# Graph attention on one core: own rows fetched earlier, and one slot in seven of layer 0 scored by two engines

## The chip, the cores and the metric

One Trainium2 chip; the kernel uses one of its cores. A core has TensorE (PE, the matrix engine; its weight loads are listed as PEld), VectorE (DVE), ScalarE (ACT), GpSimd (POOL, which here only issues indirect DMAs) and SyncE (SP, which issues plain DMAs). Each engine works off its own instructions in the order in which they were built. The metric is the device time of one execution in microseconds.

## The reference, cut to what matters

Eight batches of 2048 nodes with 256 channels pass two graph attention layers that share a sparse adjacency matrix; each layer's output is added to its input and normalised.

```python
# layer 0, leaky_relu slope 0.2
h1, h2, h3 = inp @ W1, inp @ W2, inp @ W3
e = einsum('bnd,bmd->bnm', h1, h2)
e = where(adj > 0, leaky_relu(e), -1e12)
x = layernorm(x + relu(softmax(e) @ h3))
# layer 1: e[n, m] = leaky(e_src[n] + e_dst[m]) with 4 heads of 64, elu in place of relu
```

A node has some 17 neighbours of 2048, so the kernel gathers neighbour rows and never forms the full matrix. With A = W1 W2ᵀ the logit of node n and neighbour m is (x[n] A) · x[m], and the weighted sum is taken over rows of x, and multiplied by W3 afterwards.

## The kernel before, in words

**Units.** The nodes are sorted by degree and cut into 16 tiles of 128. The batches are taken in two halves of four. One tile of one half in one layer is a *unit*: 32 units for layer 0 (first half, tiles 15 down to 0, then the second half), 32 for layer 1. A unit of tile t has K = `SLOTS[t]` neighbour slots, from 12 (tile 15) to 36 (tile 0, which is cut into two parts of 18); the 32 units of layer 0 have 596 slots.

**What is done for a layer 0 unit.**
- `list_job` and `neighbours` (first half only) turn a row of the adjacency matrix into indices.
- `chunk_job` gathers neighbour rows, `gather` being an indirect DMA issued by POOL (L196), one for each slot: 128 rows of 4 x 256 float32 into a ring `s` of 16 buffers with two slots each. A buffer is free when PE has used its second slot.
- `before0` gathers the unit's own rows into `xo`, a pool of two buffers. SP copies them to `xr`, a pool of three buffers, for the residual (L531); PE transposes them (`transposed`, L417), ACT copies the transpose out of PSUM (L419), PE multiplies by A (`projected`, L427), and ACT copies the result to `g` (L542).
- `logits0` makes, for each slot and each of the four batches, one dot product of a 256-element row with `g`. It is one DVE instruction with a sum (L562), which the profile shows as two, the product and a read of the accumulator. After all slots of a part come the leaky relu (L575), the mask, the maximum (L580), the subtraction (L581), the exponential on ACT (L582), the sum (L585) and the division (L588).
- `sums0` makes, for each slot, four diagonal matrices on ACT (`dg`, L659; four buffers of them) and lets PE multiply the slot's rows by them, accumulating in PSUM (`add_slot`, L639).
- `after0` copies the sum out (`hs`, L674), transposes it (L417, L419), multiplies by W3, adds the residual (DVE, L699), normalises (statistics on DVE, L384; logarithm and exponential of `z` on ACT, L395 and L396; L407), stores, and projects for layer 1 (L723, L731).

All PSUM tiles other than the accumulators come from one pool, `ps`, of four buffers: transposes, projections, and small things.

**Order.** Python generators are advanced by `tick`: each tick first issues what gathers the ring allows, then takes up to two steps of the logits of a later unit, then of the starts (`before0`), ends (`after0`) and lists. POOL runs in exactly that order (`manual_schedule` for Pool). The order of the other engines' instructions is set by the scheduler of the tile framework, from dependencies and its own estimates, when the program is built; on the chip each engine then keeps it. While unit j is summed, the logits of unit j+1 are made, and the start of unit j+3 is queued when half of unit j is summed:

```python
for share in sums[u.layer](u):
    ahead[0] -= share
    left -= share
    tick(left + units[min(j + 1, len(units) - 1)].K + LEAD)
    if not begun and left <= u.K / 2 and j + 3 < len(units):
        begun = True
        v = units[j + 3]
        starts.append(before[v.layer](v))
```

The lines of layer 1 that the profile names are L774 to L886 and L840 and are not touched by the change.

Of the kernel before, what the change touches and what calls it, by code (L numbers as in the profile page):

```python
# [11 lines left out]
F32 = mybir.dt.float32  # L12
BF16 = mybir.dt.bfloat16
# [3 lines left out]
AF = mybir.ActivationFunctionType  # L17
ALU = mybir.AluOpType
# [4 lines left out]
P = 128  # L23
# [106 lines left out]
def fast_path(  # L130
# [24 lines left out]
    nc = tc.nc  # L155
    B, N, C = x.shape
    NT = N // P
    KC = C // P
    HB = B // 2
    HC = HB * C  # L160
    HG = HB * H
    HW = HC // 2
# [7 lines left out]
    xop = ctx.enter_context(tc.tile_pool(name="xown", bufs=2))  # L170
# [7 lines left out]
    sp = ctx.enter_context(tc.tile_pool(name="small", bufs=4))  # L178
# [3 lines left out]
    def ps_tile(name):  # L182
        return ps.tile([P, 512], F32, tag="ps", name=name)
# [4 lines left out]
    def ring_tile(name):  # L188
        return ring.tile([P, CHUNK * 2 * QW], F32, tag="ring", name=name)

    def wide_tile(name):
        return wp.tile([P, 2 * QW], F32, tag="t", name=name)

    def gather(dst, table, index):

        nc.gpsimd.indirect_dma_start(  # L196
            out=dst, out_offset=None, in_=table, in_offset=AT(ap=index, axis=0),
            bounds_check=table.shape[0] - 1, oob_is_err=False,
        )
# [12 lines left out]
    xg = [tc.dram_tile([N, HC], F32, name=f"xg_{h}") for h in range(2)]  # L212
# [18 lines left out]
    for it in range(NT):  # L231
        r = ring_tile(f"adj_{it}")
# [54 lines left out]
    for it in range(NT):  # L287
        if it % 2 == 0:
            nc.vector.tensor_scalar(
                junk1, keys, key[:, it : it + 1], 0.0, ALU.is_gt, ALU.add,  # L290
                accum_out=rank[:, it : it + 1],
# [23 lines left out]
    order = const.tile([P, NT], I32, tag="order", name="order")  # L315
# [15 lines left out]
    for r in range(2):  # L331
        rr = slice(64 * r, 64 * r + 64)
        pr = ps_tile(f"ps_half_{r}")[:, :NT]
# [78 lines left out]
    def transposed(src, name, dst):  # L412

        for i in range(2):
            pt = ps_tile(f"ps_t_{name}_{i}")
            for j in range(4):
                nc.tensor.transpose(pt[:, ts(j, P)], src[:, ts(4 * i + j, P)], ident)  # L417
            yield
            nc.scalar.copy(dst[:, ts(i, 512)], pt)  # L419
        yield  # L420

    def projected(srcT, weight, name, evict):
        for i in range(2):
            pp = ps_tile(f"ps_p_{name}_{i}")
            for j in range(2):
                for k in range(KC):
                    nc.tensor.matmul(  # L427
                        pp[:, ts(j, C)],
                        lhsT=srcT[:, ts((2 * i + j) * KC + k, P)],
                        rhs=weight[:, k, :],  # L430
                        start=(k == 0),
                        stop=(k == KC - 1),
                    )
            yield
            evict(i, pp)
        yield

    class Unit:
        def __init__(self, layer, h, t):
            self.layer, self.h, self.t = layer, h, t  # L440
            self.K = SLOTS[t]
            self.name = f"{layer}_{h}_{t}"

            n = self.K if self.K <= RING * CHUNK * 3 // 4 else -(-self.K // 2)
            self.parts = [(k, min(n, self.K - k)) for k in range(0, self.K, n)]
            self.chunks = [[] for _ in self.parts]
            self.p = [None] * len(self.parts)
            self.ps = [None] * len(self.parts)

            self.m, self.s = [], []  # L450
            self.ready = False


# [68 lines left out]
        listed[t] = True  # L522


    def before0(u):
        xo = xop.tile([P, HC], F32, tag="xo", name=f"xo_{u.name}")
        gather(xo, xg[u.h][:, :], order[:, u.t : u.t + 1])
        u.xr = xrp.tile([P, 2, HW], F32, tag="xr", name=f"xr_{u.name}")
        for r in range(2):
            for c in range(2):  # L530
                nc.sync.dma_start(  # L531
                    u.xr[64 * c : 64 * c + 64, r, :], xo[64 * r : 64 * r + 64, ts(c, HW)]
                )
        for _ in range(4):
            yield
        xT = wide_tile(f"xT_{u.name}")
        yield from transposed(xo, f"x_{u.name}", xT)
        while scored[0] < u.index - 1:
            yield
        u.g = gp.tile([P, HC], F32, tag="g", name=f"g_{u.name}")  # L540
        yield from projected(
            xT, w.A, f"g_{u.name}", lambda i, pp: nc.scalar.copy(u.g[:, ts(i, 512)], pp)  # L542
        )
        u.ready = True

    def logits0(u):

        while not u.ready:
            yield 0
        for i, (k0, K) in enumerate(u.parts):  # L550
            n, o = f"{u.name}_{i}", offs[u.t] + k0
            e = ep.tile([P, HB, K], F32, tag="e", name=f"e_{n}")
            for k in range(K):
                c, s = divmod(k, CHUNK)
                while len(u.chunks[i]) <= c:
                    yield 0
                while clock[0] < u.chunks[i][c][2] + 3:
                    yield 0
                rows = u.chunks[i][c][0]
                for b in range(HB):  # L560
                    jt = sp.tile([P, C], BF16, tag="j", name=f"j_{n}_{k}_{b}", bufs=1)
                    nc.vector.tensor_tensor_reduce(  # L562
                        out=jt,
                        in0=rows[:, s, ts(b, C)],
                        in1=u.g[:, ts(b, C)],
                        scale=1.0,
                        scalar=0.0,
                        op0=ALU.mult,
                        op1=ALU.add,
                        accum_out=e[:, b, k : k + 1],  # L570
                    )
                yield 1
            p = e
            wide = [P, HB, K]
            nc.vector.scalar_tensor_tensor(p, e, ALPHA, e, ALU.mult, ALU.max)  # L575
            nc.vector.tensor_tensor(
                p, p, neg[:, o : o + K].unsqueeze(1).to_broadcast(wide), ALU.add
            )
            m = sp.tile([P, HG], F32, tag="m1", name=f"m_{n}")[:, :HB]
            nc.vector.tensor_reduce(m, p, AX.X, ALU.max)  # L580
            nc.vector.tensor_tensor(p, p, m.unsqueeze(2).to_broadcast(wide), ALU.subtract)  # L581
            nc.scalar.activation(p, p, AF.Exp)  # L582
            yield 0
            sm = sp.tile([P, HG], F32, tag="s1", name=f"s_{n}")[:, :HB]
            nc.vector.tensor_reduce(sm, p, AX.X, ALU.add)  # L585
            if len(u.parts) == 1:
                nc.vector.reciprocal(sm, sm)
                nc.vector.tensor_tensor(p, p, sm.unsqueeze(2).to_broadcast(wide), ALU.mult)  # L588
            u.m.append(m)
            u.s.append(sm)  # L590
            u.p[i] = p
            yield 0
# [321 lines left out]
    units = [Unit(0, h, t) for h in range(2) for t in up]  # L914
# [19 lines left out]
    for j, u in enumerate(units):  # L934
        u.index = j
    before = (before0, before1)
    logits = (logits0, logits1)
    sums = (sums0, sums1)
    after = (after0, after1)
# [7 lines left out]
    def finish(u):  # L947
        yield from after[u.layer](u)
# [6 lines left out]
    def tick(limit):  # L955
        pump()
        while late and late[0][0] <= clock[0]:
            late.popleft()[1]()
        for _ in range(2):
            if ahead[0] < limit:  # L960
                ahead[0] += next(stream, 0)
        for queue in queues:
            for _ in range(min(len(queue), 2)):
                if queue and next(queue[0], queue) is queue:
                    queue.popleft()
        clock[0] += 1
# [5 lines left out]
    for j, u in enumerate(units):  # L972
        begun = False
        if 0 < j and j + 2 < NT:
            lists.append(neighbours(up[j + 2]))
        if j == NT:
            ends.append(checks())
        while len(ends) > 1:
            tick(0)
        if 2 <= j < 10:  # L980
            b, i = divmod(j - 2, 2)
            n = ts(i, N // 2)

            nc.gpsimd.dma_start(xg[1][n, ts(b, C)], x[HB + b, n])
        left = float(u.K)
        for share in sums[u.layer](u):
            ahead[0] -= share
# [6 lines that stand above are left out]
        ends.append(finish(u))  # L994
# [300 lines left out]
```

## Time and profile before

| | us |
|---|---|
| median of 5 runs (lowest to highest) | 2593.92 (2588.98 to 2598.82) |
| time of the profiled execution | 2593.16 |
| its span, from the first to the last instruction | 2591.0 |
| busy: PE / DVE / ACT / POOL | 1807.5 / 2148.8 / 1442.3 / 1538.1 |
| granted TensorE clock, mean | 0.856 |

The stages by time in the span: preparation up to about 110 us; layer 0, first half of the batches, from 110 to about 850; layer 0, second half, to about 1600; layer 1 to the end. Inside each half the units grow from 12 slots to 36. Busy time in six stretches:

| stretch (us) | length | PE | DVE | ACT | POOL |
|---|---|---|---|---|---|
| 0 to 110 | 110 | 13.2 | 74.8 | 52.4 | 38.2 |
| 110 to 300 | 190 | 133.0 | 171.2 | 93.9 | 111.5 |
| 300 to 820 | 520 | 424.3 | 472.1 | 320.8 | 289.3 |
| 820 to 900 | 80 | 57.3 | 62.5 | 45.6 | 38.0 |
| 900 to 1400 | 500 | 405.6 | 375.1 | 298.6 | 238.0 |
| 1400 to 1600 | 200 | 158.1 | 156.0 | 128.5 | 113.0 |

How the views are read. A line of the *groups* view gives line, engine, operation, output and input tiles, shapes and count; then the busy time of all, the mean of one in ns, and the idle time of the engine just ahead of them with what ended it. A line of the *waits* view reads "engine and line <- what it waited for: us in total, times, longest us". In the *timeline* a line is start, duration, engine, instruction, and in brackets the idle time before it with what ended that. "issue" means that the profile shows no wait.

### The profile page before, as it was taken

The page shows a single profiled execution, that of the slowest core. Times are in us where ns is not written, and L with a number is a line of the kernel's source. Part 1 is how long each engine was busy: PE and PEld are TensorE (multiplying, and loading weights), DVE is VectorE, ACT ScalarE, POOL GpSimd, SP SyncE. Part 2 cuts the span into 40 slices and gives each one's busy share as a digit, 9 for nine tenths or more (in the row PEclk, how much of TensorE's full clock was granted, in tenths as well). Part 3 has the DMA queues.
Part 4 walks back from the last instruction along what each step waited for, and adds up shares of the span by engine and source line. Part 5 has one row for each costly group of instructions (what it writes and reads, how often), then busy time and mean ns, then how long its engine had stood idle before and what let it go on. Part 6 is the DMA issues. An engine that isn't in the chain of part 4 may idle for free. (4 is left out here: it accounts for less than half of the span.)

```text
span 2591.0 us, 52231 instructions
## 1 busy us (share of the span) xinstructions
PE 1807.5 (70%) x16675; PEld 984.7 (38%) x16675; DVE 2148.8 (83%) x7073; ACT 1442.3 (56%) x4849; POOL 1538.1 (59%) x1486
## 2 busy tenths in 40 slices
PE   1168787878778788787888878756465666664674
PEld 0145454545555455454555544222121212221221
DVE  6799799899989776777788885788888788888896
ACT  6246475656566555565666656554356546643455
POOL 3475455555555443545455565677677777776774
PEclk9578898989889898898898989878788788887877
DMA  9897787888885676767787868898899999987993
GB/s 383 274 339 271 258 310 266 298 292 275 290 276 185 211 225 212 266 225 241 247 263 275 268 202 281 306 354 298 294 349 348 344 335 364 349 315 270 330 350 110
DMA packets 249419, 734.92 MB, mean 284 GB/s; under 512 B 63200, under 2 KB 72544, under 8 KB 246704
## 3 DMA queue, kind: packets, MB, share of 16 engines
q0 software_dynamic: 192512, 645.89, 70.6%
q1 hardware_dynamic: 55360, 84.44, 9.6%
q8 instruction: 135, 2.21, 0.3%
q10 hardware_dynamic: 1264, 1.18, 0.1%
q14 instruction: 148, 1.21, 0.1%
HBM read 708.35 MB, written 76.09 MB: 303 GB/s over the span
## 5 line engine op out<-in xcount | busy, mean ns | idle before, releaser
L562 DVE CUSTOM_DVE_ANT_0 j<-s,g 128x256 bf16<-128x256 f32 x2384 | 1007.8, 423 | 195.0 <-DMA s<-xg,idx 125.7
L196 POOL DMA_INDIRECT s<-xg,idx x596 | 637.5, 1070 | 617.4 <-PE acc L639 393.3
L639 PE MATMUL acc<-s,ident 64*64 64x512 f32 x4768 | 607.7, 660 | 355.0 <-issue 298.0
L639 PE MATMUL acc<-s,dg 64*64 64x256 f32 x9536 | 701.6, 416 | 184.1 <-ACT dg L659 173.0
L196 POOL DMA_INDIRECT s<-qg,idx x596 | 610.5, 1024 | 241.0 <-issue 132.5
L659 ACT ACTIVATE dg<-twice,e 128x64 f32<-128x64 f32 x2384 | 617.2, 337 | 105.3 <-PE acc L639 99.2
L840 DVE TENSOR_TENSOR s<-s,p 128x2048 f32<-128x2048 f32 (+1 forms) x260 | 574.1, 2230 | 0.0
L639 PEld LDWEIGHTS acc<-s,dg 64*64 64x64 f32 x9536 | 380.3, 143 | 445.3 <-ACT dg L659 253.5
L639 PEld LDWEIGHTS acc<-s,ident 64*64 64x64 f32 x4768 | 207.9, 149 | 747.3 <-issue 596.7
L836 ACT ACTIVATE s<-s,e 128x64 f32<-128x64 f32 x1408 | 342.6, 334 | 49.3 <-DVE e L804 38.9
L395 ACT ACTIVATE z<-st,roots 128x4 f32<-128x4 f32 x64 | 19.1, 298 | 404.2 <-DVE st L384 404.2
L562 DVE DVE_READ_ACCUMULATOR2_ANT e<- 128x1 f32 x2384 | 194.2, 81 | 0.0
L204 POOL DMA_INDIRECT out_dram<-o,oidx x128 | 129.3, 1010 | 66.7 <-ACT o L407 31.2
L774 DVE TENSOR_TENSOR e<-s,own 128x32 f32<-128x32 f32 (+1 forms) x306 | 56.0, 186 | 121.4 <-DMA s<-qg,idx 118.2
L417 PE MATMUL ps_t_x<-ident,xo 128*128 128x128 f32 x256 | 55.5, 359 | 126.5 <-DMA xo<-xg,order 126.5
L723 PE MATMUL ps_q<-wqs,x1T 128*128 128x264 f32 x512 | 136.3, 403 | 0.7 <-ACT x1T L419 0.7
L427 PE MATMUL ps_p_h<-w_sb,hT 128*128 128x256 f32 x512 | 130.2, 398 | 6.1 <-ACT hT L419 6.1
L427 PE MATMUL ps_p_g<-A,xT 128*128 128x256 f32 x512 | 130.9, 401 | 0.1
L427 PEld LDWEIGHTS ps_p_h<-w_sb,hT 128*128 128x128 f32 x512 | 94.2, 194 | 41.5 <-issue 13.3
L407 ACT ACTIVATE o<-xr,nmr,rstd 128x256 f32<-128x256 f32 x128 | 66.5, 589 | 77.4 <-DVE nmr L403 69.8
L427 PEld LDWEIGHTS ps_p_g<-A,xT 128*128 128x128 f32 x512 | 97.7, 199 | 29.8 <-issue 8.5
L723 PEld LDWEIGHTS ps_q<-wqs,x1T 128*128 128x128 f32 x512 | 97.5, 197 | 27.8 <-issue 7.3
(138 smaller groups left out, 1472.6 us busy)
## 6 DMA issues: line engine op xcount, KB each, us to landing
adj<-in_adj_dram SPq DMA_DIRECT2D x16, 1024.0 KB
xr<-xo SPq DMA_DIRECT2D x128, 128.0 KB
x1s<-y SPq DMA_DIRECT2D x32, 512.0 KB
xr<-x1s SPq DMA_DIRECT2D x32, 512.0 KB
s<-xg,idx POOLq DMA_INDIRECT x596
s<-qg,idx POOLq DMA_INDIRECT x596
edges<-adj SPq DMA_DIRECT2D x16, 512.0 KB
xg<-in_x_dram SPq DMA_DIRECT2D x4, 2048.0 KB
```

The source lines that it names most:

```text
L196: nc.gpsimd.indirect_dma_start(out=dst, out_offset=None, in_=table, in_offset=AT(ap=index, axis=0), bounds_check=table.shape[0] - 1, oob_i ...
L204: ins = nc.gpsimd.indirect_dma_start(out=table, out_offset=AT(ap=index, axis=0), in_=src, in_offset=None)
L407: nc.scalar.activation(dst[:, b, :], y[:, b, :], AF.Identity, bias=nmr[:, b : b + 1], scale=rstd[:, b : b + 1],)
L417: nc.tensor.transpose(pt[:, ts(j, P)], src[:, ts(4 * i + j, P)], ident)
L427: nc.tensor.matmul(pp[:, ts(j, C)], lhsT=srcT[:, ts((2 * i + j) * KC + k, P)], rhs=weight[:, k, :], start=(k == 0), stop=(k == KC - 1),)
L562: nc.vector.tensor_tensor_reduce(out=jt, in0=rows[:, s, ts(b, C)], in1=u.g[:, ts(b, C)], scale=1.0, scalar=0.0, op0=ALU.mult, op1=ALU.add, ...
L639: nc.tensor.matmul(out, lhsT=lhsT, rhs=rhs, start=(k == 0 and j == 0), stop=(k == K - 1 and (j == 1 or diag is None)), tile_position=(64 * ...
L659: nc.scalar.activation(diag[:, b, :], twice, AF.Copy, scale=u.p[i][:, b, k : k + 1])
L723: nc.tensor.matmul(pq[:, : C + 2 * H], lhsT=x1T[:, ts(i * KC + k, P)], rhs=w.sqs[:, k, j * H : j * H + CD + H], start=(k == 0), stop=(k == ...
L774: nc.vector.tensor_tensor(e[:, c * CHUNK : c * CHUNK + ns, :].rearrange("p s (b g) -> p s b g", b=HB), rows[:, :ns, :].rearrange("p s (b w ...
L836: nc.scalar.activation(v[:, a, g, :], v[:, a, g, :], AF.Copy, scale=pv[:, a, g : g + 1])
L840: nc.vector.tensor_tensor(v, v, pv.unsqueeze(3).to_broadcast([P, n * HB, H, D]), ALU.mult)
```

## The change

Two edits, both in layer 0. First, the gather of a unit's own rows moves out of `before0` into a function of its own, `own_rows`, that the main loop calls for unit j+3 ahead of the first sum of unit j, where `before0` was queued at the middle of unit j. Everything else of `before0` stays there. The first three units still gather in `before0`. Second, for slots 3, 10, 17 (`k % 7 == 3`) of each part, DVE no longer makes four dot products with a sum; it makes two plain products of 512 elements into two PSUM tiles of the pool `ps`, and ACT reads them in four copies of 256 elements whose accumulator output is the sum.

```diff
+    def own_rows(u):
+        u.xo = xop.tile([P, HC], F32, tag="xo", name=f"xo_{u.name}")
+        gather(u.xo, xg[u.h][:, :], order[:, u.t : u.t + 1])
+
     def before0(u):
-        xo = xop.tile([P, HC], F32, tag="xo", name=f"xo_{u.name}")
-        gather(xo, xg[u.h][:, :], order[:, u.t : u.t + 1])
+        if u.xo is None:
+            own_rows(u)
+        xo = u.xo
...
                 rows = u.chunks[i][c][0]
+                if k % 7 == 3:
+
+                    for r in range(2):
+                        pr = ps_tile(f"pr_{n}_{k}_{r}")
+                        nc.vector.tensor_tensor(
+                            pr, rows[:, s, ts(r, HW)], u.g[:, ts(r, HW)], ALU.mult
+                        )
+                        for j in range(2):
+                            b = 2 * r + j
+                            ja = sp.tile([P, C], BF16, tag="ja", name=f"ja_{n}_{k}_{b}", bufs=1)
+                            nc.scalar.activation(
+                                ja, pr[:, ts(j, C)], AF.Copy, accum_out=e[:, b, k : k + 1]
+                            )
+                    yield 1
+                    continue
                 for b in range(HB):
...
             nc.gpsimd.dma_start(xg[1][n, ts(b, C)], x[HB + b, n])
+        if j + 3 < 2 * NT:
+
+            own_rows(units[j + 3])
         left = float(u.K)
```

By the built order 86 of the 596 slots take the new way: 344 pairs of DVE instructions go, 172 products and 344 ACT sums come. On POOL an own-rows gather stands 6 to 18 slot gathers earlier than before (for most units 7 to 12), except for the fourth unit, whose gather now stands first of all POOL's gathers, ahead of the first adjacency list. On PE the transposes of the own rows keep their places among the sums to within a slot, except in the third and fourth unit.

More of the change, by code (lines that the diff above doesn't have):

```diff
@@ L450, in __init__ @@
             self.m, self.s = [], []
+            self.xo = None
             self.ready = False
```

## The prediction

> **What bounds the kernel now.** I read the busy time by stretches first, then the waits of PE, DVE and ACT inside two of them, then the timeline at one wait. Layer 1 (1600 us to the end) keeps its order on every engine, so what is at stake lies between 95 and 1600 us.
>
> Two stretches; the columns are window, length, then busy time and count of PE, PEld, DVE, ACT, POOL, then clock and DMA share:
>
> ```profile
> 300.00:820.00 520.00, 424.30 (x4401) 275.31 (x4400) 472.07 (x2267) 320.81 (x1126) 289.30 (x272) 0.89 0.81 275
> 900.00:1400.00 500.00, 405.60 (x3928) 264.26 (x3928) 375.06 (x1708) 298.58 (x997) 237.99 (x227) 0.91 0.73 242
> ```
>
> The waits in 300 to 820 us:
>
> ```profile
> ACT z L395 <- DVE st L384: 104.3, 12, 13.5
> PE acc L639 <- ACT dg L659: 85.2, 19, 9.7
> ACT dg L659 <- PE acc L639: 33.5, 30, 1.9
> ACT e L582 <- DVE e L581: 33.4, 10, 10.1
> DVE j L562 <- DMA s<-xg,idx: 15.9, 20, 1.7
> PE ps_t_x L417 <- DMA xo<-xg,order: 10.3, 3, 4.6
> ```
>
> DVE is busy 91% and leads: ACT stands 138 us waiting for DVE's statistics and logits, PE stands 85 us behind ACT. This stretch is **bound by DVE**.
>
> The waits in 900 to 1400 us:
>
> ```profile
> DVE j L562 <- DMA s<-xg,idx: 91.1, 58, 7.3
> PE ps_t_x L417 <- DMA xo<-xg,order: 60.9, 12, 7.0
> ACT dg L659 <- PE acc L639: 49.3, 43, 1.9
> ACT z L395 <- DVE st L384: 43.8, 11, 7.0
> PE acc L639 <- ACT dg L659: 36.5, 26, 3.4
> ```
>
> Here DVE is busy only 75%, and waits for gathered rows; these wait for ring buffers that PE frees. PE's 405.6 busy, 60.9 waiting for own rows and 36.5 for diagonals make 503 of 500 us: nothing else is in PE's time. This stretch is **bound by PE's queue**, with 12% of it spent on own rows that came late. One such wait:
>
> ```profile
> 1007.52 1.04 POOL L196 DMA_INDIRECT xo<-xg,order  x1 [0.30 <-issue]
> ...
> 1016.37 1.09 PE L417 MATMUL ps_t_x<-ident,xo 128*128 128x128 f32 x4 [5.86 <-DMA xo<-xg,order]
> ```
>
> POOL issues the gather at 1007.5; PE, in order, has been standing before the transposes for 5.9 us when the rows are there 8.9 us after the issue.
>
> **Edit 1, own rows earlier.** PE waits 126.5 us for `xo` in all, 21 times. The first two (13.9 and 24.6 us, at 109 and 140 us) are the start-up, whose gathers are not moved ahead; 88.0 us are left: 60.9 in 900 to 1400, 10.3 in 300 to 820, some 13 in 110 to 300, 4 after 1400. At its new place a gather stands right behind one that POOL issued, in 900 to 1200, 20 to 28 us before the old `xo` issue (979.7 against 1007.5, for example); the longest of these waits is 7.0, so all should go. POOL must then wait for the buffer: for the four copies to `xr` of the unit two before. In this trace those stand at least 11 us ahead of the new places (963.5 against 979.7 here), so behind it on POOL nothing is held. The moved gather takes its 1.04 + 0.30 us of POOL either way.
>
> What is worth how much: in 900 to 1400, with 60.9 us less, DVE's 375 us stand in 439 (85%), so DVE and the diagonals get part of it; I take 50. In 300 to 820 DVE hides PE's waits: 5 of 10.3. Elsewhere 8 of 17. Together **-63**, bounds 0 and -88. At the start, the fourth unit's gather now stands ahead of the first list: 1.3 us of POOL and 512 KB, 1.5 us at the 350 GB/s of that stretch, on the path to the first index: **+2** (0 to 3).
>
> **Edit 2, on DVE.** Rows (groups by form; busy, mean ns | idle before):
>
> ```profile
> L562 DVE CUSTOM_DVE_ANT_0 j<-s,g 128x256 bf16<-128x256 f32 x2384 | 1007.8, 423 | 195.0 <-DMA s<-xg,idx 125.7 <-ACT g L542 5.4
> ...
> L731 ACT COPY q<-ps_q 128x264 f32<-128x264 f32 x128 | 48.0, 376 | 31.6 <-PE ps_q L723 31.1
> ...
> L680 ACT ACTIVATE hs<-acc,fs 128x256 f32<-128x256 f32 x8 | 3.1, 474 | 4.7 <-DVE fs L622 4.7
> L258 ACT ACTIVATION_READ_ACCUMULATOR junk<-adj 128x1 f32 x16 | 3.0, 186 | 0.0
> ...
> L873 DVE TENSOR_TENSOR v<-v,v 128x512 f32<-128x512 f32 x4 | 2.7, 684 | 0.0
> ```
>
> A dot with its accumulator read starts every 0.43 (busy time over count, 300 to 820) to 0.47 us (timeline at 1002): 1.72 to 1.87 for a slot. A product of 512 takes 684 ns, 0.64 (L867, 8 in 5.1 us busy) to 0.68 from one to the next; writing to PSUM costs hardly more (L799, 128x304 into PSUM, 483 ns; L789, same size into SBUF, 476). So 1.28 to 1.37 in its place, 0.35 to 0.6 saved, I take 0.5, x86 = 43 us. It counts where DVE leads: 43 of the 86 slots lie in 300 to 820 and after 1400, **-22** (0 to -52).
>
> New waits of DVE. By the built order 94 of the 172 products wait for ACT to free a PSUM tile, so many of slot 10's and 17's products stand at the end of their part; in 4 of the 34 parts nothing at all lies between them and the leaky relu, in some 8 more only one or two dots. There DVE waits while ACT sums: four sums of 0.6 less the second product, 2 us; about 20 us in all, dots and lists queued behind. Some 8 of it falls where DVE leads: **+8** (0 to +30). At the turn to the second half, the products of slot 10 of unit (1, tile 14) now stand behind the statistics and checks (about 885 us); its exponential was at 862, its first diagonal at 893.4. With ACT's sums it is late next: **+5** (0 to +12).
>
> **Edit 2, on ACT.** No row has 256 elements from PSUM with an accumulator. Lower bound 0.37 + 0.19 (L731 and the read), upper 0.47 + 0.19 (L680 and the read): 0.56 to 0.66, I take 0.6; x344 = 206 us more ACT. In 900 to 1400, 27 slots, 65 us: 49.3 us of ACT's waiting for PE to free a diagonal absorb most, the rest delays diagonals that PE waits for: **+20** (0 to +65). In 300 to 820, 33 slots, 79 us: taking each sum's new place in ACT's order and the times of its neighbours in this trace, DVE would deliver the product some -1 to +14 us after ACT gets there, in the middle 1.7. So ACT waits, sums 2.4 us, and the diagonals behind come later; PE has slack to DVE there: **+10** (0 to +30).
>
> [...]
>
> **Sum.** -63 + 2 - 22 + 8 + 5 + 20 + 10 = -40 on the profiled 2593.16 (2591.0 of span and 2.2 around it), so 2553. The median of the runs, 2593.92, lies 0.8 above: 2554.
>
> **Rivals.**
> - *Both in full* (15%). The own-row waits go entirely (-88 + 2), DVE's 22 count, ACT's sums hide in its idle 40%: 2485 with no new wait at all, 2510 with those of DVE at +13 and of ACT at +12. For it: PE's account of 900 to 1400 is complete, ACT is idle enough. Against: ACT's idle time is waiting in order, not free room.
> - *The wait moves* (12%). What PE no longer waits for rows it waits for diagonals (36.5 us in that stretch already) or DVE becomes the bound there: 63 shrinks to 20, 2596 in the sum; if the ACT terms are half as well, 2581. Between: about 2589. Against: DVE and ACT are at 75% and 60% there.
> - *ACT becomes the bound: slower* (22%). Place: diagonals behind the sums. In 300 to 820 ACT has 321 busy + 79 + 138 waiting for DVE = 538 of 520 if its waits for DVE stay whole, and in 900 to 1400 all 65 fall on PE: +18, +65, and 10 slots after 1400 +12, with the waits of DVE at +25 and +5, against -63 + 2 - 22: 2635 at worst; with three quarters of the first three, 2611, which I take. It decides once more than 60% of those 95 us are felt.
> - *It doesn't do what it says* (4%): the scheduler's buffer wait holds the own rows as late as before; only edit 2 stays, about 2600. The order on POOL speaks against it.
>
> **How the numbers follow.** My forecast (47%) is 2554, its own range 2527 to 2583. The range that should hold 8 in 10 takes in most of "both in full" and the near part of "slower": 2505 to 2612. A measurement of this kernel can tell about 0.2% (5.2 us) from no change. Faster: 47 + 15 + 5 of "moves" = 67%; same: 6 + 2 = 8%; slower: 22 + 1 + 2 = 25%.
>
> **What would show it.** Edit 1: the wait of PE for `xo` falls from 126.5 to about 40 us, and DVE's wait for rows in the second half shrinks with it. Edit 2: L562 falls by 344 pairs; the products show 0.69 us, the sums 0.37 to 0.47 with a read of 0.19; DVE gains a wait for ACT at the leaky relu of 10 to 30 us; PE's wait for `dg` grows from 173 by less than 40. I am wrong if that wait grows by 80 or more, if ACT's waits for products are as long as the sums themselves, or if POOL waits for `xr` copies ahead of own rows.

## The result and the profile after

| | before | after |
|---|---|---|
| median, us (runs) | 2591.7 (78) | 2596.66 (41) |
| lowest to highest | 2579.55 to 2602.5 | 2586.47 to 2605.0 |
| span of the profiled execution | 2591.0 | 2591.2 |
| busy DVE / ACT | 2148.8 / 1442.3 | 2104.6 / 1566.8 |

The ratio is 1.0018, with a 95% interval of 1.0011 to 1.0025: 0.2% slower, where 2554 had been forecast. The two profiled executions are equally long, but inside they are not alike. The table follows the end of each unit's last diagonal on ACT (us from the start, from the traces):

| unit (half, tile) | before | after | difference |
|---|---|---|---|
| (0, 15) | 174.7 | 180.6 | +5.9 |
| (0, 7) | 500.0 | 511.4 | +11.3 |
| (0, 3) | 685.2 | 717.9 | +32.8 |
| (0, 0) | 854.3 | 894.6 | +40.3 |
| (1, 12) | 1011.5 | 1035.9 | +24.3 |
| (1, 6) | 1282.4 | 1276.6 | -5.7 |
| (1, 0) | 1588.5 | 1590.6 | +2.1 |

So 40 us are lost in the first half, most of it in its large units, 46 are won between the turn and unit (1, 6), and 8 are lost again in the large units at the end.

The windows of the profile after, for the same two stretches (length, then busy time and count of PE, PEld, DVE, ACT, POOL, then clock, DMA share and GB/s):

```profile
300.00:820.00 520.00, 419.40 (x4080) 259.62 (x4075) 426.40 (x1949) 350.81 (x1301) 268.02 (x255) 0.93 0.78 269
900.00:1400.00 500.00, 424.62 (x4159) 272.58 (x4163) 390.95 (x1668) 355.22 (x1306) 260.19 (x245) 0.93 0.78 261
```

Between 300 and 820 us no engine is fuller than before but ACT: DVE fell from 472.1 to 426.4, and less was done in that time (PE's matmuls 4401 to 4080). Between 900 and 1400 all engines are busier.

Since less was done between 300 and 820, the same work has to be compared: from the end of unit (0, 12) to that of (0, 1), first before, then after, each with DVE's wait for rows in it.

```profile
290.80:785.60 494.80, 403.70 (x4124) 263.26 (x4127) 447.18 (x2146) 306.76 (x1071) 275.06 (x259) 0.89 0.83 286
DVE j L562 <- DMA s<-xg,idx: 18.5, 21, 1.9
...
299.70:822.90 523.20, 422.61 (x4112) 261.30 (x4108) 428.34 (x1958) 353.43 (x1312) 269.16 (x256) 0.93 0.78 268
DVE j L583 <- DMA s<-xg,idx: 70.2, 43, 7.6
```

These units take 28.4 us longer. DVE is busy 18.8 us less in them and waits 51.7 us longer for gathered rows.

The waits of the kernel after in 300 to 820 us:

```profile
ACT ja L576 <- DVE pr L570: 109.7, 29, 10.4
DVE j L583 <- DMA s<-xg,idx: 68.2, 42, 7.6
PE acc L660 <- ACT dg L680: 42.4, 42, 3.6
ACT dg L680 <- PE acc L660: 15.6, 16, 1.9
ACT z L395 <- DVE st L384: 10.9, 7, 3.9
```

The first line is new: ACT stands before a sum whose product DVE has not made, 3.8 us each time. DVE's wait for gathered rows was 15.9 and is 68.2, so that DVE loses more to waiting than it saves in work. The wait for own rows is gone.

The same in 900 to 1400 us:

```profile
DVE j L583 <- DMA s<-xg,idx: 59.0, 44, 5.0
ACT ja L576 <- DVE pr L570: 58.8, 27, 4.6
PE acc L660 <- ACT dg L680: 48.9, 31, 3.7
ACT z L395 <- DVE st L384: 28.7, 10, 5.9
ACT dg L680 <- PE acc L660: 13.5, 16, 4.7
```

Here the 60.9 us of PE's wait for `xo` are gone, and DVE's wait for rows fell from 91.1 to 59.0, as forecast.

The groups by form show each operation at the price that was forecast (busy, mean ns | idle before):

```profile
L576 ACT ACTIVATE ja<-pr 128x256 bf16<-128x256 f32 x344 | 130.9, 380 | 251.5 <-DVE pr L570 248.9
...
L570 DVE TENSOR_TENSOR pr<-s,g 128x512 f32<-128x512 f32 x172 | 112.8, 693 | 14.1 <-DMA s<-xg,idx 9.5 <-ACT q L752 4.4
...
L576 ACT ACTIVATION_READ_ACCUMULATOR ja<-pr 128x1 f32 x344 | 68.5, 199 | 0.0
```

What was not forecast stands behind the last bar of the first line: 248.9 us of ACT waiting for products, more than the 199 that the sums take.

The timeline of the kernel after around two such stops, while unit (0, 3) is summed and the logits of (0, 2) are made (start, duration, engine, instruction, idle time before it with its cause):

```profile
675.51 0.38 ACT L576 ACTIVATE ja<-pr 128x256 bf16<-128x256 f32 x1 [10.44 <-DVE pr L570]
...
678.17 1.11 PE L417 MATMUL ps_t_h<-ident,hs 128*128 128x128 f32 x4 [10.94 <-ACT hs L695]
...
681.50 0.99 POOL L196 DMA_INDIRECT s<-xg,idx  x1 [10.21 <-PE acc L660]
...
688.72 0.43 DVE L583 CUSTOM_DVE_ANT_0 j<-s,g 128x256 bf16<-128x256 f32 x1 [7.64 <-DMA s<-xg,idx]
...
691.57 1.29 DVE L570 TENSOR_TENSOR pr<-s,g 128x512 f32<-128x512 f32 x2
692.29 0.38 ACT L576 ACTIVATE ja<-pr 128x256 bf16<-128x256 f32 x1 [4.35 <-DVE pr L570]
...
694.57 4.11 PE L660 MATMUL acc<-s,dg 64*64 64x256 f32 x32 [2.29 <-ACT dg L680]
```

Read it as a ring. ACT, in order, has stood 10.44 us before a sum whose product was late, with the copies of `hs` (677.53) and the next diagonals (678.48) behind it. PE therefore stands 10.94 us at the transposes of `hs`. POOL's gather has waited 10.21 us for a ring buffer that PE frees, and goes out at 681.50. Its rows, by the count of the slots, are those for which DVE stands 7.64 us, until 688.72. So DVE's next product is late too, ACT stands again, 4.35 us, and PE 2.29 us behind it.

### The profile page after: what moved, and what is told of

Its sections match the earlier page's. It is cut to its first block, busy times and chain, and to the rows that moved or that the text cites. A ratio compares the mean times of both kernels' runs of the same rounds, so it can differ in the third digit from the quotient of the medians.

```text
span 2591.2 us, 52332 instructions
## 1 busy us (share of the span) xinstructions
PE 1827.5 (71%) x16675; PEld 972.3 (38%) x16675; DVE 2104.6 (81%) x6557; ACT 1566.8 (60%) x5537; POOL 1535.4 (59%) x1486
## 5 line engine op out<-in xcount | busy, mean ns | idle before, releaser
L583 DVE CUSTOM_DVE_ANT_0 j<-s,g 128x256 bf16<-128x256 f32 x2040 | 862.3, 423 | 218.7 <-DMA s<-xg,idx 166.9
L660 PE MATMUL acc<-s,dg 64*64 64x256 f32 x9536 | 722.1, 410 | 154.8 <-ACT dg L680 144.3
L680 ACT ACTIVATE dg<-twice,e 128x64 f32<-128x64 f32 x2384 | 631.3, 342 | 36.3 <-PE acc L660 35.3
L576 ACT ACTIVATE ja<-pr 128x256 bf16<-128x256 f32 x344 | 130.9, 380 | 251.5 <-DVE pr L570 248.9
L395 ACT ACTIVATE z<-st,roots 128x4 f32<-128x4 f32 x64 | 19.0, 296 | 256.0 <-DVE st L384 255.9
L744 PE MATMUL ps_q<-wqs,x1T 128*128 128x264 f32 x512 | 143.2, 417 | 36.6 <-ACT q L752 13.5
L583 DVE DVE_READ_ACCUMULATOR2_ANT e<- 128x1 f32 x2040 | 166.2, 81 | 0.0
L744 PEld LDWEIGHTS ps_q<-wqs,x1T 128*128 128x128 f32 x512 | 99.1, 202 | 70.3 <-ACT q L752 15.9
L570 DVE TENSOR_TENSOR pr<-s,g 128x512 f32<-128x512 f32 x172 | 112.8, 693 | 14.1 <-DMA s<-xg,idx 9.5
```

The costliest lines, as they stand in the source:

```text
L570: nc.vector.tensor_tensor(pr, rows[:, s, ts(r, HW)], u.g[:, ts(r, HW)], ALU.mult)
L576: nc.scalar.activation(ja, pr[:, ts(j, C)], AF.Copy, accum_out=e[:, b, k : k + 1])
L583: nc.vector.tensor_tensor_reduce(out=jt, in0=rows[:, s, ts(b, C)], in1=u.g[:, ts(b, C)], scale=1.0, scalar=0.0, op0=ALU.mult, op1=ALU.add, ...
L660: nc.tensor.matmul(out, lhsT=lhsT, rhs=rhs, start=(k == 0 and j == 0), stop=(k == K - 1 and (j == 1 or diag is None)), tile_position=(64 * ...
L680: nc.scalar.activation(diag[:, b, :], twice, AF.Copy, scale=u.p[i][:, b, k : k + 1])
L744: nc.tensor.matmul(pq[:, : C + 2 * H], lhsT=x1T[:, ts(i * KC + k, P)], rhs=w.sqs[:, k, j * H : j * H + CD + H], start=(k == 0), stop=(k == ...
```

## The experiments

Theory: **the wait in order.** ACT's stops before products tie PE's diagonals of this unit to DVE's logits of the next, and PE's ring buffers tie DVE to PE. Rivals: ACT's added **time** by itself; the PSUM **tiles** that products hold; a loss by **edit 1**. Two groups ran on two slower chips: on that of a1_own, a2_split and a4_short before takes 2700.65 us, on that of c0_before to b2_second 2702.07. So all are compared by their ratio to before on the same chip (95% interval in brackets).

**Own rows alone, the split alone, and short sums**

```diff
 a1_own: without the split
-                if k % 7 == 3:
...
 a2_split: without the early gather
-        if j + 3 < 2 * NT:
-            own_rows(units[j + 3])
 a4_short: both edits
-                                ja, pr[:, ts(j, C)], AF.Copy, accum_out=e[:, b, k : k + 1]
+                                ja[:, :8], pr[:, j * C : j * C + 8], AF.Copy, accum_out=e[:, b, k : k + 1]
```

> Edit 1 alone: own rows ahead, all slots by DVE's dots. Theory (the two edits work against each other: own rows gain in the second half, edit 2 loses as much in the large units of the first half): 2540 to 2555, the sums of unit (first half, tile 0) end within 6 us of before (854 us), those of (second half, tile 6) some 45 us earlier than before (1282 us); PE's waits for own rows fall to about 45 us. Rival (own rows ahead cost the first half by pushing neighbour gathers back): the first half ends 25 us or more late in this kernel too, and the time is 2580 or more.

> Edit 2 alone: one slot in seven by DVE's products and ACT's sums, own rows as before. Theory: slower, 2630 to 2645, and the first half's sums end 30 to 45 us later than before; PE's waits for own rows stay over 100 us. Rival (the loss in the first half is edit 1's): 2585 to 2600 and the first half ends within 10 us of before.

> Both edits, but ACT sums only the first 8 of 256 elements of each batch, so the logits of those slots are wrong; all waits, tiles and instruction counts stay, ACT has some 0.2 us less for each of 344 sums, 70 us in all. If ACT's time is what the change loses by: 2570 or less. If the waits in ACT's order (for DVE's products) and for PSUM tiles are: within 12 us of both edits together, 2585 to 2600, with ACT's wait for products as long as or longer than the 249 us there.

Measured: own rows alone 0.9851 (0.9827 to 0.9876), the split alone 1.014 (1.0118 to 1.0161), short sums 0.9995 (0.998 to 1.001). The product of the first two is 0.999: the change is a gain of 1.5% and a loss of 1.4%. The short sums with their reads still take 127.9 us of ACT, where the full ones take 199.4; the third that is gone bought at most 0.4%. So this bounds the price of the sums' length only loosely: by it, all 199 us could be worth up to some 1.1% (an estimate, 0.4% times 199 over 71). The split alone missed two of its marks: PE waited 80.8 us for own rows, where over 100 was expected, and the first half ended 17 us later than in the trace of c0_before, where 30 to 45 was expected.

**Before and after on the second slower chip, sums one slot later, and the split in the second half only**

```diff
 b1_late: the sums are issued behind the next slot's dots
-                            nc.scalar.activation(
-                                ja, pr[:, ts(j, C)], AF.Copy, accum_out=e[:, b, k : k + 1]
-                            )
+                        late.append((k, r, pr))
...
+                if late:
+                    summed(n, e, late)
 b2_second
-                if k % 7 == 3:
+                if u.h == 1 and k % 7 == 3:
```

> The kernel before, unchanged, for a trace from the chip on which the next kernels run. The marks of the units of layer 0 (the end of each unit's last diagonal on ACT) should stand as in the first trace, apart from one factor for the chip. If the loss of some 40 us by the end of the first half (854 to 895 us in the first two traces) is a property of the kernels and not of one execution, it must show against the changed kernel here too.

> The changed kernel, unchanged, beside the others of this group. Ratio to before 1.002 (0.999 to 1.005). Against the trace of before from this chip: some 30 to 40 us late at the end of the first half, all of it caught up in units (1, tile 12) to (1, tile 6), a few us late after the last units of layer 0.

> Both edits, but ACT's sums of a product are issued one slot later, behind the next slot's dots in program order (at once if it is the last slot of its part). Theory of order: what edit 2 costs is that ACT stops in order before a product that DVE has not yet made (249 us of waits), with the diagonals behind it. A slot of DVE's work (1.7 us) between product and sum then takes much of it away: ACT's wait for products falls from 249 to below 120 us, PE's wait for diagonals falls, and the time falls by 8 to 30 us against the changed kernel, ratio to before 0.990 to 0.999. Rival, tiles: what it costs is that the products hold two of the four PSUM tiles that PE fills for its projections and transposes. They are then held a slot longer, PE's waits at the transposes and projections for ACT grow, and the time rises by 5 to 25 us, ratio 1.004 to 1.012. Rival, DVE's own cost: neither matters, same time as the changed kernel within 4 us.

> Own rows ahead as in the change; products with sums on ACT only in the second half of layer 0 (half of the slots), none in the first. If the loss lies in the first half, where DVE leads, as the marks of the units say: the end of the first half comes as in own rows alone, and the ratio to before is 0.985 to 0.990, no more than 0.004 above own rows alone (0.985). Rival, the loss is spread evenly over the slots: half of edit 2's 1.4 per cent stays, ratio 0.992. Rival, the loss of the first half is edit 1's (gathers of own rows ahead of the list on POOL): the end of the first half is then still 30 us late against before, and the ratio is 0.997 or more.

Measured: after again 1.0033 (1.0017 to 1.0049); one slot later 1.0022 (1.0005 to 1.0038); split in the second half only 0.9924 (0.9902 to 0.9945). By the unit marks on that chip, after stands 0.6 us ahead at unit (0, 7) and 28.6 late at (0, 0), so the loss does lie in the large units; own rows alone, from the other slower chip, are 4.3 late at (0, 0). But half of the split slots gave half of the loss, as the rival of an even spread said: beside own rows alone, the split in the second half loses 27 us from the end of unit (1, 7) on, and hardly 2 before (its trace is that of the slowest of its six runs, so 27 is rather too much). So it is large units, of both halves. The one-slot delay did not do what was expected of it (0.990 to 0.999) and told nothing: in the built order its sums stood only 0.04 slots of diagonals later on ACT, in the mean, because the scheduler had set them back.

**One suspected cost at a time**

```diff
 d1_time: own rows, all dots on DVE, and ACT sums its own g tile
+                if k % 7 == 3:
+                    for b in range(HB):
...
+                        nc.scalar.activation(
+                            ja, u.g[:, ts(b, C)], AF.Copy, accum_out=nkey[:, b : b + 1]
+                        )
 d2_wait: own rows, all dots on DVE, and ACT copies one number that a dot has written
+                if k % 7 == 3:
...
+                    nc.scalar.copy(ja, e[:, HB - 1, k : k + 1])
 d4_tiles3: own rows alone, one PSUM tile less
-    ps = ctx.enter_context(tc.tile_pool(name="ps", bufs=4, space=PSUM))
+    ps = ctx.enter_context(tc.tile_pool(name="ps", bufs=3, space=PSUM))
 b3_late4: both edits, sums issued four slots later
-                if late:
+                if late and k >= late[0][0] + 4:
```

> Own rows ahead, and DVE makes all dots as before; at every seventh slot ACT makes four sums of 256 elements of its own g tile from SBUF, whose results nothing uses (extra work, the output stays the reference's). So ACT has the time of edit 2's sums in the same places of its order (some 200 us), but waits for nothing of DVE, takes no PSUM tile, and DVE saves nothing. Own rows alone gave 0.985 of before, both edits 1.002 to 1.003. Theory, the wait in order costs: 0.985 to 0.991. Rival, ACT's time costs by itself, since diagonals stand behind it: 0.998 to 1.008. That the shorter sums (8 of 256 elements) bought only 0.3 per cent speaks for the first.

> Own rows ahead, and DVE makes all dots as before; at every seventh slot ACT copies the one number that the slot's last dot has just written (86 copies of 128x1, some 0.2 us each, whose results nothing uses). So ACT waits in order for DVE at the same 86 places as in the change, with hardly any time of its own (some 17 us), and no PSUM tile. Theory, the wait in order costs: most of the gap between 0.985 and 1.003 shows here, ratio 0.994 to 1.006, ACT's wait for these dots is 100 to 200 us, and DVE's wait for gathered rows grows to 130 us or more. Rivals, ACT's time or the PSUM tiles cost: 0.985 to 0.989.

> Own rows ahead, nothing of edit 2, and three PSUM tiles in place of four for projections, transposes and their like. Rival of tiles (the products hold PSUM tiles that PE needs): the loss of one tile all the time is at least as bad as two tiles held for 2 to 10 us at 86 slots, ratio 0.993 or more. Theory, the wait in order costs: PE's waits behind evictions grow a little, ratio 0.985 to 0.991.

> Both edits, with ACT's sums issued four slots behind their product (at the end of the part if that comes first). Four slots of DVE are some 7 us, about the length of ACT's longer waits for products (7 to 10 us). Theory, the wait in order costs: ACT's wait for products falls from 171 to below 60 us, and if the tiles cost nothing the time falls by 15 to 40 us against the changed kernel, ratio 0.988 to 0.998. Rival of tiles: products now hold two of four tiles for 8 us and more; PE and DVE wait for ACT to free them, ratio 1.005 to 1.02. Since one slot of delay gave 1.002 in place of 1.003, both may work against each other.

Measured: time alone 0.9859 (0.9841 to 0.9876), the wait alone 1.002 (1.0004 to 1.0036), a tile less 0.9866 (0.9843 to 0.9888), four slots later 0.9988 (0.9975 to 1.0002). The wait alone makes the whole loss. The groups and waits of the wait alone:

```profile
L580 ACT COPY ja<-e 128x1 f32<-128x1 f32 x86 | 16.3, 189 | 289.7 <-DVE e L568 289.6
```

```profile
POOL s L196 <- PE acc L648: 496.7, 197, 15.2
...
ACT ja L580 <- DVE e L568: 289.6, 71, 13.6
...
DVE j L568 <- DMA s<-xg,idx: 123.9, 86, 8.5
```

And the groups and waits of ACT's time alone:

```profile
L581 ACT ACTIVATE ja<-g 128x256 bf16<-128x256 f32 x344 | 142.6, 415 | 6.4
```

```profile
POOL s L196 <- PE acc L651: 435.2, 195, 15.9
...
DVE j L568 <- DMA s<-xg,idx: 87.5, 71, 7.9
```

86 copies of one number, 16.3 us of ACT, cost 1.6% (1.002 against 0.986, some 42 us), because ACT stops 71 times for DVE. They stand where the change has its sums (0.24 slots of diagonals earlier, in the mean). With them gathers wait longer for PE (496.7 against 435.2) and DVE longer for rows (123.9 against 87.5): the ring again. ACT's wait for the dots is even longer than the 100 to 200 us expected. It is not that the copies rearranged the other work: by the tiles' names, only 14 of the 4855 other instructions on ACT, 32 of 7074 on DVE and none on POOL stand at another place than with own rows alone. That the ring is the way from the stops to the time is read from these waits; no run changed the ring itself.

344 sums with 207 us of ACT (142.6 and 64.7 for the reads) cost nothing that shows, and only 6.4 us of idle time stand before them. But they are not in the change's places, as the expectation has it: since they need nothing but `g`, they stand 19.6 slots of diagonals earlier in ACT's order, in the mean, most of them behind a copy of `g` or `q`. So this run shows that ACT has room for them there; what the sums' time costs in the change's own places was not measured alone.

The fourth kernel had again not moved its sums: 0.24 slots in the built order, a wait for products of 241.9 us, where below 60 was expected.

**Sums that really stand later.** A tie makes the four sums follow the last diagonal that was emitted by the time of the fourth or sixth slot behind the product. The third kernel is edit 1 for the second half only.

```diff
 e1_behind4; e2_behind6 has 6 for 4
+                if late and k == late[0][0] + 4:
+                    with tc.issue_after(last_dg[0].ins):
+                        summed(n, e, late)
 f1_own_second: no split, and
-        if j + 3 < 2 * NT:
+        if NT <= j + 3 < 2 * NT:
```

> Both edits; where at least four more slots of the part follow, ACT's sums are tied behind the last diagonal emitted by the time of the fourth slot after the product. In the built order the sums then stand 1.7 slots of diagonals later on ACT than in the changed kernel, in the mean; in the two earlier delays (one slot and four slots, without the tie) they had stood 0.04 and 0.24 slots later, that is, they had not moved. Theory, the wait in order costs: ACT's wait for products falls from 249 to 120 to 190 us, and the ratio to before falls from 1.002 to 0.992 to 0.998. Rival: a wait that is moved comes back at another place (PE or DVE waiting for the PSUM tiles that the products hold longer), ratio 1.000 to 1.006.

> The same with six slots: the sums stand 2.6 slots of diagonals later than in the changed kernel, in the mean. Theory: ACT's wait for products falls further, to 70 to 150 us, ratio 0.987 to 0.996 and below that of four slots. Rival: ratio at or above that of four slots, with longer waits of PE or DVE for a PSUM tile.

> Edit 1 alone, and only for the units of the second half of layer 0: the first half gathers its own rows as before, so neither the fourth unit's gather ahead of the first list nor any other of the first half is moved. Own rows alone ended the first half 4 to 6 us late against before on the same chip. If that is edit 1's price there, this gives 0.983 to 0.985, some 3 us less than own rows in both halves (0.985 to 0.987); if it is only spread between executions, the two agree within 0.002; if the gain of the second half needs the first half's gathers too, 0.988 or more.

Measured: four slots 0.9866 (0.9845 to 0.9886), six slots 0.979 (0.9765 to 0.9814), own rows in the second half alone 0.977 (0.975 to 0.9789). Waits of the kernel with six slots:

```profile
DVE j L593 <- DMA s<-xg,idx: 113.0, 99, 4.1
...
ACT ja L559 <- DVE pr L583: 108.6, 34, 9.9
```

ACT's wait for products goes 248.9, 157.2, 108.6, and the ratio goes 1.002, 0.987, 0.979, with the same instructions and the PSUM tiles held longer: from a product's start to the last read of it 2.1, 4.0 and 5.8 us, in the mean. Both gains are larger than the theory's expectation. The first half ends 5.7 us late in place of 40.3. The rival of tiles falls here for the second time: PE's waits for a tile that a sum had still to read, 36.5 us in after, are 5.4 with six slots. Here too the other work kept its order but for 183 instructions on ACT and 24 on DVE. And all the sums' time, less what DVE saves, costs nothing here: 0.979 stands below own rows alone. Own rows in the second half alone did better than any of its expectations (0.983 at the best).

**Both better halves, and only slots with room behind them**

```diff
 g1_both: e2_behind6 with own rows as in f1_own_second
-        if j + 3 < 2 * NT:
+        if NT <= j + 3 < 2 * NT:
 g2_room: and
-                if k % 7 == 3:
+                if k % 7 == 3 and k + 6 < K:
```

> The two better halves together: own rows ahead for the second half's units alone, and the sums tied six slots behind their products. Own rows for the second half alone gave 0.977; the tie brought both edits from 1.002 to 0.979. If the two gains are separate (the tie lets DVE's 43 us of edit 2 count where DVE leads, own rows of the second half count where PE leads): 0.968 to 0.975. If DVE's saving is worth nothing once own rows are early, as before (own rows with the tie gained only 5 to 15 us over own rows alone): 0.975 to 0.979.

> The same, but only those slots are split that have six more slots behind them in their part (58 of 86); the others stay four dots on DVE. No sum is then issued at once behind its product, and the sums stand 4 slots of diagonals later in the mean. Theory, the wait in order costs: ACT's wait for products falls from some 109 us to below 40, and DVE saves 29 us in place of 43: ratio at or below that of all 86, 0.965 to 0.973. Rival, DVE's saving counts for more than the waits that are left: 0.973 to 0.980, above that of all 86.

Measured: 0.9769 (0.9747 to 0.979) and 0.9802 (0.9781 to 0.9823). Beside own rows of the second half, the split costs nothing and gains nothing: 0.9769 against 0.977. With fewer split slots ACT's wait for products fell from 92.8 to 34.8 us, yet the time did not fall; of the two expectations the rival's holds, at its upper edge: what DVE saves on the 28 slots counts for no less than the waits that they bring. Saving and stops are not separated here. The best versions, g1_both and f1_own_second, are 2.3% faster than before; f1_own_second is a condition in the main loop and needs no split.

**Edit 1 in the first half only**

```diff
 h1_own_first: no split, and
-        if j + 3 < 2 * NT:
+        if j + 3 < NT:
```

> Edit 1 alone, and only for the units of the first half of layer 0 (the thirteen after the start); the second half gathers its own rows as before. Own rows in both halves gave 0.985, own rows in the second half alone 0.977. If the first half's moved gathers cost what lies between, this is slower than before: 1.004 to 1.010. If they only cost the 6 to 8 us by which the first half ended later in the traces: 1.001 to 1.004. If the difference lay in something else (another chip, another state of the second half at its start), the same as before within 0.001, or faster, by the 5 us that the prediction gave for PE's waits in 300 to 820 us.

Measured: 1.0019 (1.0003 to 1.0035), the second of the three expectations. Here the moved gathers cost instead of gaining. The first half ends 7.6 us late (861.9 against 854.3). A wait of this kernel in 110 to 860 us:

```profile
POOL s L196 <- DVE some L506: 69.3, 11, 12.9
```

In before this wait of the gathers for a list of neighbours, which DVE makes only in this half, is 43.9 us, and with own rows of the second half alone 44.9. DVE's wait for rows goes from 23.3 to 33.5. That the moved gather is what makes the lists late is a reading, not tried.

## Why the prediction was wrong

Its sum was -40; the median rose by 5. By the run of own rows alone, edit 1 was taken for 22 us too much and edit 2 for 22 too little.

1. **Edit 1, -63 + 2.** The wait went as forecast: PE's 126.5 us for `xo` became 44.0 (about 40 was said). In the second half alone own rows are worth 60 us (0.977 of some 2592), where the prediction's 50 for 900 to 1400 and part of 8 elsewhere stood: right. In the first half 5 us and part of those 8 were to be won; moved alone, they cost 5. Edit 1 in both halves is worth 39 us (0.9851). So this term was too large by some 22 us. Moved alone, the halves give -60 and +5, together -55; why both at once give only -39 stays open. Own rows in both halves ran on a slower chip, and on the others only with one more alteration (0.986, 0.987).

2. **DVE's saving, -22.** The saving itself is there: 43 forecast, 44.2 in DVE's busy time, 693 ns for a product. What it is worth was wrong too. "This stretch is bound by DVE" took 91% of busy time for the bound; in the change as built, DVE, 18.8 us less busy from (0, 11) to (0, 1), waited 51.7 us more for rows, and none of the saving is seen. With the stops made rarer, it shows as nothing beside own rows of the second half (0.9769 against 0.977), and as some 16 us beside own rows in both (0.979 against 0.985). In both, stops are left (92.8 and 108.6 us of ACT's waiting); what the saving is worth without any was not measured.

3. **New waits of DVE at the leaky relu, +8, and the turn, +5.** About 20 us of wait were forecast, 9.6 are there (of DVE for `ja` at L596). Small and no part of the error; the turn was not measured by itself.

4. **ACT's sums, +20 and +10: the step that failed.** Their duration was right: 380 and 199 ns, where 0.37 to 0.47 and 0.19 us were said; at 692 us one starts every 0.50 us, less than the 0.6 that was taken. The prediction priced their time; the cost that it left out is that ACT stops. d2_wait has the stops with 16.3 us of ACT in place of 199 and nothing saved on DVE, and loses 42 us; e2_behind6 has all the sums and fewer stops (34 against 83), and loses nothing against own rows alone (0.979 against 0.985). The prediction saw the lag ("-1 to +14 us", "in the middle 1.7") and dropped it with "PE has slack to DVE there". In 300 to 820 ACT stopped 29 times for 3.8 us, and the large units of the first half alone lost 29 us by the marks ((0, 7) to (0, 0)), where +10 stood. The split as a whole was to cost 21 us (-22 + 8 + 5 + 20 + 10); alone it cost 36 (0.014 of 2592), and added to own rows in both halves 43 (1.0018 against 0.9851).

The rival "ACT becomes the bound" named the place, diagonals behind the sums, but priced the sums' time on top of ACT's old waits; d2_wait shows that the new stops make the loss without that time. Of the signs it gave for being wrong, "ACT's waits for products are as long as the sums themselves" came true (248.9 against 199), "PE's wait for `dg` grows" did not: it fell from 173.0 to 144.3. That sign was badly chosen: the loss of the large units shows in DVE's and POOL's waits, further around the ring: in 300 to 820 us DVE's wait for rows went from 15.9 to 68.2, and POOL's for ring buffers that PE frees from 102.1 to 129.9.

The PSUM tiles do not decide here: one tile less changed nothing (0.9866 against 0.9851), and sums that hold their tiles longer (5.8 us against 2.1) were faster (0.979 against 1.002).

## What to carry to other kernels

Splitting one step over two engines added a stop on the second wherever the first was late (here 83 stops and 248.9 us of ACT); price the stop and what is queued behind it, and not the instructions alone. Before calling an engine the bound because it is 91% busy, follow one of its short waits around: if it waits for a buffer that the next engine frees, less work for it can come back as waiting (here 18.8 us less busy, 51.7 us more waiting). And look in the built order whether an instruction stands where it was meant to: the sums of b1_late and b3_late4 had not moved, and those of d1_time had.

## What the runs showed that was not expected

- 86 copies of one number on ACT, 189 ns each, cost some 42 us, while 344 sums with 207 us of ACT, some 20 slots of diagonals earlier and waiting for nothing, cost none.
- ACT's waits for DVE do not measure the harm by their sum: before, statistics (404.2) and the exponential (101.1) make 505 us; after, with the products, 546 (255.9 + 41.1 + 248.9). We take it that what counts is where in the order of the diagonals the stop falls; no run moved a stop of the same length.
- The same program took some 2592 us on some chips and 2701 and 2702 on two others; the traces of before show granted clocks of 0.856 and 0.871. In these two traces of before, layer 0 ends 25 us apart (1588.5 and 1614.0) and the rest of the 115 us lies in layer 1, with 308 to 351 GB/s against 286 to 316 in windows of 200 us from 1600 to 2400. Ratios agreed better than times: the changed kernel 1.0018 and 1.0033.
